# One stream over the quarters in layer 0, whole tiles only in the test of adj, a shorter root, closing algebra by threes

## The chip, the cores and the metric

The kernel runs on one core of a Trainium2 chip. A core has a matmul engine (TensorE, PE in the profile), a vector engine (VectorE, DVE), a scalar engine for activation functions (ScalarE, ACT), a general engine (GpSimd, POOL) and a sync engine (SyncE, SP) that here only issues DMAs. [...] The metric is the device time of one launch in microseconds (us); lower is better. TensorE's clock can be lowered by the chip; in the profiled execution it was granted .984 of full speed on average.

## The reference

There are 4096 nodes with 64 features, a matrix adj of 4096 x 4096 entries of 0 or 1 (a share of .0078 is 1), and four layers of the form x = x + GNN(relu(layernorm(x))):

- Layer 0: a decayed sum over neighbours. `rank` is the running count of neighbours along a row of adj, `k = min(deg, 100)`, `pos = rank - (deg - k)`, and neighbour j counts with `0.5 ** (k - pos)`: the last neighbour has weight 1, the one before 1/2, and so on. `out = w @ (h @ weight) + bias`.
- Layer 1: attention with hyperbolic (Lorentz) linear maps. Such a map computes `h = x @ W.T + b`, `time = sigmoid(h[0]) * exp(scale) + 1.1`, and stretches the other 63 components by `sqrt((time^2 - 1) / sum of squares)`. `att = adj * sigmoid((2 + 2 * qm @ k.T) / att_scale + att_bias)`, then `att @ h`, divided by the root of its Lorentz norm.
- Layer 2: two gated graph convolutions one after the other: `m = adj @ (x @ W)`, then the gates r, z, n of a GRU cell from m and x.
- Layer 3: `adj @ (gamma * X)` and `adj @ (gamma - 1)` for points X of a ball, their quotient, and a chain of norms, artanh and tanh of each node, after which the result is added to x.

The kernel's fast path holds adj in 8-bit floats, which is exact for entries of 0 and 1. So it must also find out whether all entries are 0 or 1: it counts the others, and a general path runs if there are any.

## The kernel before

`fast_kernel` (L791) does the work. Columns of the transposed adj are taken in four quarters of 1024 nodes (`NQ = 4`), each in 32 blocks of 128 rows (`NB = 32`).

**adj comes in twice.** `load0` (L1104; the DMA at L1109) has GpSimd's queue read a tile of 128 x 1024 fp32 and write it as 8-bit floats, 128 KB, to its fixed place in `A8`; 128 tiles in all, 12 before the first turn and then one per turn, 12 ahead. Every later layer reads `A8`. A second full read, on SP's queue, serves the test alone: `checks` (L1060) loads fp32 tiles, and one VectorE operation per tile counts the entries that are neither 0 nor 1. Until layer 2, tiles are halves (128 x 512, 256 KB) in buffers of the pool `b2`, which the rest of the kernel's work shares, four in flight; from layer 2 on there are also wholes (128 x 1024, 512 KB) in the four buffers of `b4`. An order is fixed: the DMAs of a queue are issued in the order written, and so are the tests on VectorE.

**Layer 0.** `stream0(q)` (L1111) is called once per quarter. It goes through the 32 blocks from the last to the first, in pairs. For each block and each half of 512 columns, `turn` (L1117) adds to a running count in PSUM by two matmuls with triangular matrices (`cnt <- A, fupd` and `cnt <- A, ftri`), and the count is turned into a weight tile `w` by ScalarE (three of four) or VectorE (one of four). The sums `acc` over neighbours are matmuls of `w` with the node features, split in a 128-wide part `hm` and a 64-wide `lo`, and stand up to four pairs behind the counts (`waiting`). At the end of a quarter the waiting sums are emptied, `evac` (L1010) copies the sums out at once (two ScalarE copies, two VectorE adds), and only then does the next quarter begin; `post0` does what follows (transposing, adding to x, and the first maps of layer 1). The counts' two PSUM banks are freed at the end of the quarter too.

**Layer 1.** `stream1` (L1310) forms scores by matmul, ScalarE takes their sigmoid, VectorE multiplies with the tile of adj (`sig`), and TensorE sums. One unit of 1024 scores wide takes one of each. Keys of all four quarters must be there before the scores that use them: `k` of quarter q comes from a chain of `relu_ln` (L920), and `lorentz` (L1208) with `stretch` (L1231) twice, mostly small VectorE operations on 128 x 8 elements. All of them use `rsqrt` (L899): a guess from the bits, and three Newton steps of three operations.

**Layers 2 and 3.** Layer 2 runs matmuls of adj with features twice. Layer 3 sums over adj for eight groups u of 512 nodes, (0, 1, 2), (3, 4, 5) and (6, 7); `take3` (L1660) takes the sums of one group from PSUM, and `post3` (L1680) does the closing algebra. `summed` (L1652) hands groups to it in pairs as they come: (3, 4), (5, 0), (1, 2), and 6 and 7 alone.

**The order of the work** is written out when the kernel is built, by a planner, `Weave` (L~640 to 745). It keeps an estimated clock per engine and one for the DMAs (`dma`), and an estimated landing for each loaded tile (`land`: 1.4 us per A tile and per whole, .7 per half). Side work is given as generators in the list `work`, of which two run at a time, and `back`, which holds the tests. After each group of matmuls `draw` issues those operations that can end before TensorE's clock of the plan; `until` and `finish` force them. The estimates only set the order: on the chip engines wait for semaphores.

Engines are wrapped by the class `Engine` (L747), so nearly all operations of ACT, DVE and SP bear line L780, matmuls L946 and transposes L950. Groups in the profile are told apart by the names of their tiles.

Of the kernel before, what the change touches and what calls it, by code (L numbers as in the profile page):

```python
# [9 lines left out]
F32 = mybir.dt.float32  # L10
# [8 lines left out]
P = 128  # L19
D = 64  # L20
# [551 lines left out]
CB = 4  # L572
W0 = float(2.0 ** 27)
# [173 lines left out]
class Engine:  # L747
# [12 lines left out]
    def __getattr__(self, name):  # L760
        fn, w = getattr(self.real, name), self.weave

        def call(*args, **kw):
# [7 lines left out]
            def run():  # L771
# [5 lines left out]
                if name == "dma_start":  # L777
                    for k in outs:
                        w.land(k, 1.4 if "whole" in k else 0.7)
# [11 lines left out]
def fast_kernel(ctx: ExitStack, tc: tile.TileContext, t: dict, out: bass.AP, flag: bass.AP):  # L791
# [18 lines left out]
    b2p = ctx.enter_context(tc.tile_pool(name="fb2", bufs=24))  # L810
    b4p = ctx.enter_context(tc.tile_pool(name="fb4", bufs=4))
    small = ctx.enter_context(tc.tile_pool(name="fsmall", bufs=24))
# [18 lines left out]
    def stat(name, n):  # L831
        return small.tile([P, 2 * QB], F32, tag="st", name=name)[:, :n]
# [66 lines left out]
    def rsqrt(v, eng):  # L899

        n = v.shape[1]
        guess = small.tile([P, 2 * QB], I32, tag="st", name="guess")[:, :n]
        yield eng.tensor_scalar(guess, v.bitcast(I32), -0.5, float(0x5f3759df), op0=ALU.mult, op1=ALU.add)
        y = guess.bitcast(F32)
        for _ in range(3):
            a = stat("nt", n)
            yield eng.tensor_tensor(a, y, y, ALU.mult)
            if eng is DV:
                yield DV.scalar_tensor_tensor(a, a, -0.5, v, op0=ALU.mult, op1=ALU.mult)
                z = stat("ny", n)  # L910
                yield DV.scalar_tensor_tensor(z, a, 1.5, y, op0=ALU.add, op1=ALU.mult)
            else:
                yield eng.tensor_tensor(a, a, v, ALU.mult)
                yield eng.tensor_scalar(a, a, -0.5, 1.5, op0=ALU.mult, op1=ALU.add)
                z = stat("ny", n)
                yield eng.tensor_tensor(z, a, y, ALU.mult)
            y = z
        return y

    def relu_ln(x, dst):  # L920
# [6 lines left out]
        eng = root[0]  # L927
        yield eng.tensor_scalar(v, v, 1.0 / D, LN_EPS, op0=ALU.mult, op1=ALU.add)
        r = yield from rsqrt(v, eng)
        yield DV.scalar_tensor_tensor(dst, xc, 0.0, rows(r), op0=ALU.max, op1=ALU.mult)  # L930

    root = [DV]
# [77 lines left out]
    def evac(acc, bias=None):  # L1010
# [4 lines left out]
        for ps, (own, other) in zip(acc, sides):  # L1015
            S_.activation(mt[own, :], ps[other, :], AF.Copy)
        for ps, (own, other) in zip(acc, sides):
            if bias is None:
                V.tensor_tensor(a[own, :], ps[own, :], mt[own, :], ALU.add)
            else:  # L1020
                V.scalar_tensor_tensor(a[own, :], ps[own, :], bias[own, :], mt[own, :], op0=ALU.add, op1=ALU.add)
# [35 lines left out]
    depth = [4]  # L1057
    spare = [0]

    def checks():  # L1060

        todo = [(b, c) for c in range(NQ) for b in range(NB)]
        loaded, halves, n = [], [], 0

        def load(a, b, c, k):
            Y_.dma_start(a, adjT[b * P:(b + 1) * P, c * CW:(c + k) * CW])
            loaded.append(a)

        while todo or loaded or halves:
            while todo or halves:  # L1070
                whole = sum(a.shape[1] > CW for a in loaded)
                if whole < spare[0] and todo:
                    b, c = todo.pop(0)
                    load(b4p.tile([P, 2 * CW], F32, tag="b4", name="whole"), b, 2 * c, 2)
                elif len(loaded) - whole < depth[0]:
                    if not halves:
                        b, c = todo.pop(0)
                        halves += [(b, 2 * c), (b, 2 * c + 1)]
                    load(b2("half", (P, CW)), *halves.pop(0), 1)
                else:  # L1080
                    break
# [8 lines left out]
        r = stat("odd", 1)  # L1090
        yield DV.tensor_reduce(r, odd, AX.X, ALU.add)
# [743 lines left out]
```

## Time and profile before

| | us |
|---|---|
| three runs | 837.53, 838.41 (median), 840.33 |
| span of the profiled execution | 837.9 |
| TensorE, VectorE, ScalarE busy | 786.7 (94%), 648.4 (77%), 400.8 (48%) |
| 156 tests of halves on VectorE | 101.5, .686 each |
| 50 tests of wholes on VectorE | 59.8, 1.219 each |
| from issue to landing: half, whole, A tile | 6.6, 6.0, 13.3 (medians) |
| DMA queues, 16 engines' share of the span | 30.4% SP's main queue, 21.2% GpSimd's |

Layer 0 takes about 0 to 253 us of the span, layer 1 to 512, layer 2 to 720, layer 3 to 814, and the closing algebra the rest. How to read the profile: a row of a group names line, engine and operation, then "out<-in" by the program's tiles with shapes and the count; after the bar busy time and mean duration in ns, then how long the engine idled just before these instructions and what ended most of that. In a timeline a row begins with start and busy time, and square brackets give the wait ahead of it and what it waited for. In a list of waits, a row gives the waiting work, what it waited for, the sum in us, the count and the longest. An engine that idles off the critical path costs nothing; what counts is what TensorE waits for until its last matmul, and what VectorE does after it.

### The profile page before, as it was taken

How to read it: one execution, taken by the hardware profiler on the slowest of the kernel's cores; microseconds unless marked ns; L12 is line 12 of the kernel's file. 1: busy time of each engine (PE TensorE's matmuls, PEld its weight loads, DVE VectorE, ACT ScalarE, POOL GpSimd, SP SyncE). 2: the span in 40 equal slices, each digit the busy share in tenths (PEclk: the TensorE clock that was granted, in tenths of full speed). 3: DMA queues.
4: the chain of work that ended last, by engine and by line, in shares of the span. 5: the costliest groups of instructions: out<-in, count | busy, mean ns of one | idle time of the engine just before them, and what ended most of it. 6: DMA issues, size and time to landing. Idle time of an engine off the chain costs nothing.

```text
span 837.9 us, 12661 instructions
## 1 busy us (share of the span) xinstructions
PE 786.7 (94%) x4549; PEld 368.7 (44%) x4570; DVE 648.4 (77%) x1675; ACT 400.8 (48%) x613; POOL 69.5 (8%) x143
## 2 busy tenths in 40 slices
PE   5999979999999989999999999999999999999980
PEld 2443423433443333333333333444444444699980
DVE  6535856767688798888888888968778788775995
ACT  4655545555556657566666563122210244462342
POOL 4333232332000000000000000000000000000000
PEclk9999989999999999999999999999999999999995
DMA  9999999999943032002012125596878900000000
GB/s 133 115 146 160 174 184 206 164 179 203 198 124 105 13 105 87 24 26 84 19 51 87 39 57 194 181 314 218 289 242 311 280 26 1 1 2 2 14 22 22
DMA packets 67735, 100.58 MB, mean 120 GB/s; under 512 B 18896, under 2 KB 35280, under 8 KB 67664
## 3 DMA queue, kind: packets, MB, share of 16 engines
q1 hardware_dynamic: 47360, 79.18, 30.4%
q0 software_dynamic: 18432, 16.79, 21.2%
q10 hardware_dynamic: 1872, 3.71, 1.2%
q8 instruction: 38, 0.62, 0.3%
q14 instruction: 33, 0.27, 0.1%
HBM read 144.75 MB, written 5.24 MB: 179 GB/s over the span
## 4 chain that ended last, share of the span: by engine, by line
PE 82%; DVE 9%; DMA 5%; ACT 2%; issue 1%; SPq 0%; DVEq 0%
PE acc L946 50%; PE score L946 13%; PE cnt L946 11%; DMA half<-in_adjT 4%; PE ps_l L946 2%; DVE sig L780 2%; PE rz L946 2%; PE ih L946 2%; PE ps_t L950 1%; DVE nt L780 1%; DVE n L780 1%; DMA x<-in_x 1%; DVE ss L780 1%; ACT w L780 1%; ACT sig L780 1%
## 5 line engine op out<-in xcount | busy, mean ns | idle before, releaser
L780 ACT ACTIVATE sig<-score,fatt_add,fatt_mul 128x1024 f32<-128x1024 f32 x128 | 147.6, 1200 | 82.6 <-PE score L946 82.5
L780 DVE TENSOR_TENSOR sig<-sig,A 128x1024 f32<-128x1024 f32 x128 | 151.3, 1222 | 33.0 <-ACT sig L780 32.6
L780 ACT ACTIVATE w<-cnt 128x512 int16<-128x512 f32 x192 | 108.2, 595 | 100.1 <-PE cnt L946 99.6
L946 PE MATMUL score<-qd,kT 64*128 64x512 f32 x512 | 127.4, 615 | 0.0
L946 PE MATMUL acc<-sig,S 128*64 128x512 f32 x512 | 124.7, 606 | 1.5 <-DVE sig L780 1.5
L946 PE MATMUL acc<-A,hm 128*128 128x512 fp8e4 x512 | 115.6, 379 | 0.0
L946 PEld LDWEIGHTS <-hm 128*128 128x128 bf16 x768 | 73.3, 98 | 91.1 <-issue 12.8
L946 PE MATMUL cnt<-A,fupd 128*128 128x512 fp8e4 x248 | 96.2, 388 | 12.7 <-ACT w L780 6.4
L780 DVE SCALAR_TENSOR_TENSOR half<-half 128x512 f32<-128x512 f32 x156 | 101.5, 686 | 8.0 <-DMA half<-in_adjT 7.9
L946 PE MATMUL cnt<-A,ftri 128*128 128x512 fp8e4 x256 | 98.5, 388 | 8.1 <-DMA A<-in_adjT 8.1
L946 PE MATMUL acc<-S,A 128*128 128x196 bf16 x1024 | 88.2, 247 | 0.0
L946 PEld LDWEIGHTS <-A 128*128 128x128 fp8e4 x1024 | 87.2, 97 | 1.1 <-issue 0.8
L1109 POOL DMA_DIRECT2D A<-in_adjT x128 | 67.7, 531 | 142.5 <-DMA A<-in_adjT 138.4
L946 PEld LDWEIGHTS score<-qd,kT 64*128 64x128 f32 x512 | 44.0, 186 | 79.0 <-issue 36.1
L780 DVE TENSOR_SCALAR w<-cnt 128x512 int16<-128x512 f32 x64 | 44.3, 691 | 41.3 <-PE cnt L946 40.6
L946 PE MATMUL acc<-w,hm 128*128 128x512 bf16 x235 | 69.9, 382 | 0.7 <-issue 0.2
L946 PEld LDWEIGHTS acc<-sig,S 128*64 128x64 f32 x512 | 30.6, 136 | 80.8 <-issue 31.2
L946 PEld LDWEIGHTS <-lo 128*64 128x64 bf16 x768 | 36.9, 109 | 58.5 <-issue 36.7
L780 DVE SCALAR_TENSOR_TENSOR whole<-whole 128x1024 f32<-128x1024 f32 x50 | 59.8, 1219 | 3.0 <-DMA whole<-in_adjT 2.6
L946 PE MATMUL acc<-A,lo 128*64 128x512 fp8e4 x512 | 59.3, 380 | 0.0
L780 ACT ACTIVATE mt<-acc 64x512 f32<-64x512 f32 x32 | 18.9, 591 | 65.6 <-PE acc L946 65.2
L946 PEld LDWEIGHTS <-ftri 128*128 128x128 bf16 x256 | 25.0, 99 | 48.8 <-issue 26.9
(177 smaller groups left out, 684.4 us busy)
## 6 DMA issues: line engine op xcount, KB each, us to landing
half<-in_adjT SPq DMA_DIRECT2D x156, 256.0 KB, 6.6
whole<-in_adjT SPq DMA_DIRECT2D x50, 512.0 KB, 6.0
A<-in_adjT POOLq DMA_DIRECT2D x128, 128.0 KB, 13.3
x<-in_x SPq DMA_DIRECT2D x8, 256.0 KB, 16.6
qd<-qs SPq DMA_DIRECT2D x16, 128.0 KB, 2.7
mx<-gs SPq DMA_DIRECT2D x16, 128.0 KB, 7.3
xT<-gs SPq DMA_DIRECT2D x8, 256.0 KB, 7.0
xs<-x SPq DMA_DIRECT2D x4, 256.0 KB, 7.1
```

The costliest lines, as they stand in the source:

```text
L780: return fn(*args, **kw)
L946: nc.tensor.matmul(o, lhsT, rhs, start=start, stop=stop, skip_group_check=True)
L950: nc.tensor.transpose(o, src, ident)
L1109: nc.gpsimd.dma_start(A8[q][b // 2][:, b % 2, :], adjT[b * P:(b + 1) * P, q * 2 * CW:(q + 1) * 2 * CW])
```

## The change

- `stream0` takes all four quarters in one go. The sums of a quarter may now run on into the turns of the next one; `acc` is kept per quarter, the counts are freed per quarter, and `evac` is no longer done at once but as the first piece of `post0` (and of `post1` in layer 1), among the side work.
- Tests of adj are all of wholes: 128 tiles of 128 x 1024. They are added in the middle of quarter 0 rather than after it, with up to five in flight and, in layer 0, only while the plan's DMA clock is at most 13 us ahead of TensorE's; from the middle of quarter 3 two in flight; in layer 1 no limit by clocks; four in flight after it. Landing estimates go to 1.45 for a tile of A and .8 for other loads.
- Pools: `b2` from 24 to 20 buffers, `b4` from 4 to 6, small buffers from 24 to 22 of wider size (24 columns).
- `rsqrt` has 8 operations: the guess and two longer steps. The Lorentz maps keep `time` less 1 and do with fewer operations (15 to 11 a call). All of it stays on VectorE.
- The closing algebra goes by three: (3, 4, 5), (0, 1, 2), then 6 and 7 alone. Remaining VectorE work of the tests is issued before the last sums of groups 0 to 2; the last extra reduce of the tests is dropped.

The number of TensorE's instructions stays almost the same (8426 instead of 8424 in the two kernels' lists).

```diff
-                        w.land(k, 1.4 if "whole" in k else 0.7)
+                        w.land(k, 1.4 if "whole" in k else 0.8)
...
-    b2p = ctx.enter_context(tc.tile_pool(name="fb2", bufs=24))
-    b4p = ctx.enter_context(tc.tile_pool(name="fb4", bufs=4))
-    small = ctx.enter_context(tc.tile_pool(name="fsmall", bufs=24))
+    b2p = ctx.enter_context(tc.tile_pool(name="fb2", bufs=20))
+    b4p = ctx.enter_context(tc.tile_pool(name="fb4", bufs=6))
+    small = ctx.enter_context(tc.tile_pool(name="fsmall", bufs=22))
...
-    def rsqrt(v, eng):
+    def rsqrt(v):
         n = v.shape[1]
-        guess = small.tile([P, 2 * QB], I32, tag="st", name="guess")[:, :n]
-        yield eng.tensor_scalar(guess, v.bitcast(I32), -0.5, float(0x5f3759df), op0=ALU.mult, op1=ALU.add)
+        guess = small.tile([P, ST], I32, tag="st", name="guess")[:, :n]
+        yield DV.tensor_scalar(guess, v.bitcast(I32), -0.5, float(0x5f3759df), op0=ALU.mult, op1=ALU.add)
         y = guess.bitcast(F32)
-        for _ in range(3):
-            a = stat("nt", n)
-            yield eng.tensor_tensor(a, y, y, ALU.mult)
-            if eng is DV:
-                yield DV.scalar_tensor_tensor(a, a, -0.5, v, op0=ALU.mult, op1=ALU.mult)
-                z = stat("ny", n)
-                yield DV.scalar_tensor_tensor(z, a, 1.5, y, op0=ALU.add, op1=ALU.mult)
-            else:
-                yield eng.tensor_tensor(a, a, v, ALU.mult)
-                yield eng.tensor_scalar(a, a, -0.5, 1.5, op0=ALU.mult, op1=ALU.add)
-                z = stat("ny", n)
-                yield eng.tensor_tensor(z, a, y, ALU.mult)
-            y = z
-        return y
+        a, u, z = stat("nt", n), stat("nu", n), stat("ny", n)
+        yield DV.tensor_tensor(a, y, y, ALU.mult)
+        yield DV.tensor_tensor(u, a, v, ALU.mult)
+
+        yield DV.scalar_tensor_tensor(a, u, -10.0 / 3.0, u, op0=ALU.add, op1=ALU.mult)
+        yield DV.scalar_tensor_tensor(y, a, 5.0, y, op0=ALU.add, op1=ALU.mult)
+        yield DV.tensor_tensor(a, y, y, ALU.mult)
+        yield DV.scalar_tensor_tensor(a, a, -0.5 * (3.0 / 8.0) ** 3, v, op0=ALU.mult, op1=ALU.mult)
+        yield DV.scalar_tensor_tensor(z, a, 1.5 * 3.0 / 8.0, y, op0=ALU.add, op1=ALU.mult)
+        return z
...
         for ps, (own, other) in zip(acc, sides):
-            S_.activation(mt[own, :], ps[other, :], AF.Copy)
+            yield AC.activation(mt[own, :], ps[other, :], AF.Copy)
         for ps, (own, other) in zip(acc, sides):
             if bias is None:
-                V.tensor_tensor(a[own, :], ps[own, :], mt[own, :], ALU.add)
+                yield DV.tensor_tensor(a[own, :], ps[own, :], mt[own, :], ALU.add)
             else:
-                V.scalar_tensor_tensor(a[own, :], ps[own, :], bias[own, :], mt[own, :], op0=ALU.add, op1=ALU.add)
+                yield DV.scalar_tensor_tensor(a[own, :], ps[own, :], bias[own, :], mt[own, :],
+                                              op0=ALU.add, op1=ALU.add)
             free(ps)
...
-    depth = [4]
-    spare = [0]
+    lead = [13]
+    depth = [5]
     def checks():
         todo = [(b, c) for c in range(NQ) for b in range(NB)]
-        loaded, halves, n = [], [], 0
-
-        def load(a, b, c, k):
-            Y_.dma_start(a, adjT[b * P:(b + 1) * P, c * CW:(c + k) * CW])
-            loaded.append(a)
-
-        while todo or loaded or halves:
-            while todo or halves:
-                whole = sum(a.shape[1] > CW for a in loaded)
-                if whole < spare[0] and todo:
-                    b, c = todo.pop(0)
-                    load(b4p.tile([P, 2 * CW], F32, tag="b4", name="whole"), b, 2 * c, 2)
-                elif len(loaded) - whole < depth[0]:
-                    if not halves:
-                        b, c = todo.pop(0)
-                        halves += [(b, 2 * c), (b, 2 * c + 1)]
-                    load(b2("half", (P, CW)), *halves.pop(0), 1)
-                else:
-                    break
+        loaded, n = [], 0
+        while todo or loaded:
+            while todo and len(loaded) < depth[0] and not (loaded and weave.dma > weave.t["P"] + lead[0]):
+                b, c = todo.pop(0)
+                a = b4p.tile([P, 2 * CW], F32, tag="b4", name="whole")
+                Y_.dma_start(a, adjT[b * P:(b + 1) * P, c * 2 * CW:(c + 1) * 2 * CW])
+                loaded.append(a)
...
+    def stream0():
+
         cols = [slice(c * CW, (c + 1) * CW) for c in (0, 1)]
-
-        def turn(b):
+        cnt, acc, waiting = [], {}, []
+
+        def turn(q, b):
...
+        def sums():
+
+            if not waiting:
+                return
+            q, b, w0, w1 = waiting[0]
+            if b == NB - 1:
+                acc[q] = [one(f"acc{c}") for c in (0, 1)]
             for c in (0, 1):
-                add_hm(acc, 0, b, c, w0[c], b == NB - 1)
-            add_hm(acc, 0, b - 1, 0, w1[0], False)
-
-        def add_second(b, w0, w1):
-            add_hm(acc, 0, b - 1, 1, w1[1], False)
+                add_hm(acc[q], 0, b, c, w0[c], b == NB - 1)
+            add_hm(acc[q], 0, b - 1, 0, w1[0], False)
+            yield
+            add_hm(acc[q], 0, b - 1, 1, w1[1], False)
             for i, wt in enumerate((w0, w1)):
                 for c in (0, 1):
-                    add_lo(acc, 0, b - i, c, wt[c], b - i == 0)
-
-        waiting = []
-
-        def sums():
-
-            if not waiting:
-                return
-            item = waiting[0]
-            add_first(*item)
-            yield
-            add_second(*item)
+                    add_lo(acc[q], 0, b - i, c, wt[c], b - i == 0)
             waiting.pop(0)
+            if b == 1:
+                weave.add(post0(q, acc.pop(q)))
         def here(item):
-            part = 0, item[0] // QB
+            part = 0, item[1] // QB
             return part in DONE and weave.ready("P", names(LO[part])) <= weave.t["P"]
-        for b in range(1, NB, 2)[::-1]:
...
+        for q in range(NQ):
+            cnt[:] = [two(f"cnt{c}")[:, :CW] for c in (0, 1)]
+            for b in range(1, NB, 2)[::-1]:
...
+                if b == NB // 2 + 1:
+                    xq[q] = b2(f"x{q}")
+                    Y_.dma_start(xq[q], x_nm[:, q * QB:(q + 1) * QB, :])
+                    if q == 0:
+                        weave.add(checks(), back=True)
+                    if q == NQ - 1:
+                        load1(0)
+                        depth[0] = 2
+            for x in cnt:
+                free(x)
+        begin1()
         while waiting:
             for _ in sums():
                 weave.draw()
...
-    def post0(q, a):
+    def post0(q, acc):
         X = xq.pop(q)
+        a = yield from evac(acc, w("b0"))
...
+        t2, f = stat("t2", n), stat("f", n)
+        yield DV.scalar_tensor_tensor(t2, tm, 2.0, tm, op0=ALU.add, op1=ALU.mult)
+        yield DV.scalar_tensor_tensor(ss, ss, 1e-8, t2, op0=ALU.max, op1=ALU.mult)
+        r = yield from rsqrt(ss)
+        yield DV.tensor_tensor(f, t2, r, ALU.mult)
...
+        yield DV.tensor_scalar(o[:, :, 0], tm, 1.0, sign, op0=ALU.add, op1=ALU.mult)
...
+        while weave.back and weave.back[0][1].e == "D":
+            weave.issue(weave.back[0])
...
+        group.append((u, parts3))
+        if alone or len(group) == 3:
+            weave.add(post3(group[:]))
+            group.clear()
...
-        weave.add(post0(q, evac(acc, w("b0"))))
-        if q == 0:
-            weave.add(checks(), back=True)
+    stream0()
+    lead[0] = math.inf
+    stream1()
     depth[0] = 4
-    stream1()
-    depth[0], spare[0] = 3, 4
     gate_w = []
```

## The prediction

> **What bounds the kernel now.** I read the page first (busy times, slices, chain), then the trace by stages (windows), then TensorE's waits in layer 0, then the timeline around each, last the end.
>
> ```profile
> span 837.9 us, 12661 instructions
> PE 786.7 (94%) x4549; PEld 368.7 (44%) x4570; DVE 648.4 (77%) x1675; ACT 400.8 (48%) x613; POOL 69.5 (8%) x143
> PEclk9999989999999999999999999999999999999995
> 0.00:253.00 253.00, 229.91 (x1141) 98.61 (x1164) 168.99 (x496) 136.78 (x250) 68.58 (x135) 0.99 1.04 167
> 253.00:512.00 259.00, 255.83 (x1112) 84.46 (x1108) 221.42 (x378) 165.78 (x166) 0.00 (x0) 1.00 0.20 58
> 512.00:720.00 208.00, 207.44 (x1240) 95.08 (x1239) 170.24 (x418) 52.96 (x89) 0.46 (x4) 1.00 0.61 201
> 720.00:814.00 94.00, 93.56 (x1063) 90.59 (x1060) 73.30 (x312) 38.23 (x98) 0.46 (x4) 1.00 0.03 7
> 814.00:838.00 24.00, 0.00 (x0) 0.00 (x0) 14.41 (x75) 7.07 (x13) 0.00 (x0) 0.60 0.10 26
> ```
>
> The five lower lines are layer 0, layer 1, layer 2, layer 3 and the tail (sum, then PE, PEld, DVE, ACT, POOL; clock; DMA share; GB/s). TensorE is the bound: all but full in layers 2 and 3, 3 us short in layer 1, 23 us in layer 0, absent from the tail. Only these gaps and the tail can give time; so I ask which wait ends each.
>
> ```profile
> PE cnt L946 <- DMA A<-in_adjT: 8.1, 1, 8.1
> PE cnt L946 <- ACT w L780: 6.4, 11, 1.4
> PE cnt L946 <- DVE w L780: 6.2, 3, 4.0
> ...
> 71.95 0.38 PE L946 MATMUL cnt<-A,fupd 128*128 128x512 fp8e4 x1 [1.37 <-ACT w L780]
> ...
> 95.69 43.04 SPq L780 DMA_DIRECT2D half<-in_adjT  x18
> ...
> 112.24 0.69 DVE L780 SCALAR_TENSOR_TENSOR half<-half 128x512 f32<-128x512 f32 x1 [4.83 <-DMA half<-in_adjT]
> ...
> 113.60 0.59 PE L946 MATMUL cnt<-A,fupd 128*128 128x512 fp8e4 x1 [4.02 <-DVE w L780]
> ...
> 174.96 0.69 DVE L780 SCALAR_TENSOR_TENSOR half<-half 128x512 f32<-128x512 f32 x1 [2.45 <-DMA half<-in_adjT]
> ...
> 307.33 0.66 PE L950 MATMUL ps_t<-fident,k 128*128 128x128 f32 x4 [2.15 <-DVE k L780]
> ...
> 814.42 0.60 DVE L780 TENSOR_TENSOR n<-n,acc 128x130 f32<-128x130 f32 x2
> ...
> 830.40 0.42 DVE L780 TENSOR_TENSOR X<-X,n 128x256 f32<-128x256 f32 x1
> ```
>
> The first wait (8.1) is the start of the kernel; the diff leaves it. The 1.37 us gap at 71.95 is the turn from quarter 0 to 1 and comes again near 136 and 196. The 4.02 us gap is no arithmetic: VectorE stood 4.83 us at a test whose half tile had not landed, with `w` queued behind it. At 307.33 TensorE waits for layer 1's keys. After the last matmul a chain of small VectorE operations runs to 830.8; the output's DMA and the end take 7.1 us more.
>
> [...] `w`, whose counts were ready, stands behind the half. [...] Here the 4.02 us gap is followed by matmuls started .38 to .43 us apart until 118.9 instead of .2155; the 1.37 us gaps show nothing of it. [...] tiles of A land 1.45 us apart alone, 1.91 to 2.02 with halves queued.
>
> **Part 1, one stream over the quarters.** It removes the draining of sums and the immediate evacuation at three turns. From start to start the three boundaries lose 1.54 + .41 = 1.95 us each, 5.85 in all. The evacuation's 2 ACT copies (.59 each) and 2 VectorE adds per quarter stay, but woven between `w` evictions; I leave .3 us per turn for a late `w`. Gain 5.85 − .9 = 4.9 (bounds 0 and 5.85).
>
> **Part 2, tests of whole tiles, earlier, limited.** 156 half tests x .686 = 107.0 us of VectorE become 78 whole tests x (1.219 + .082 spacing) = 101.5: nothing on the path by itself. What counts is where a test waits. The gap at 113.60 costs 4.18 from start to start and about 2.7 at the half clock; that near 176 costs 1.65. Together 8.55. In the changed order SP issues a whole as soon as the test six before it freed a buffer; no load waits for TensorE or ScalarE any longer (halves shared the 2 KB buffers with their work). Issue to test is 5 to 6 pairs of turns, 16 to 20 us. A half landed 16.5 us after issue in the bad spot, about 8 of them in line, 2.05 us per 256 KB, so a whole takes about 4.2 us of the queue under contention, and the limit holds fewer in line. I take the whole 8.55 as gained (bounds 3, if the clock recovers but gaps of a few tenths spread; 8.55; the case of nothing gained is a rival).
>
> Its price is paid by A. Loads start about 23 us earlier: SP can issue six wholes right behind the load of x at 27.5, where the first half went at 50.6. At 28 us about 13.5 tiles of A have landed and 10.5 are used; margins from landing to use are 8.5 us at tile 16, 12.5 at 28, 16.8 at 32. With a whole beside each tile I estimate 2.5 us per tile [...] against a use of about 2 us. Until tile 30 to 38 that consumes the margin and leaves a shortage between 0 and 2.5 us; POOL's loads stay 12 ahead. I take 1.0 lost (bounds 0 and 5). The bytes up to the last A tile stay much the same, so A still ends near 223 us, needed at 240. What is left for layer 2: 74 wholes x 1.30 = 96 us of VectorE beside 208 us in which it was busy 170, instead of 37 halves and 50 wholes = 93.5: covered by TensorE's 207.44 busy of 208.
>
> **Part 3, root of 8 operations instead of 10, shorter algebra.** In layers 1 and 2 it lies beside matmuls, except for the keys at 307.33: lost there 2.44 from start to start, and .99 + .54 us at two other gaps. The key chain loses two operations in relu-layernorm and four in each of two Lorentz maps, 10 x .20 us (start to start of a 128x8 operation) = 2.0; also quarter 3's keys now stand one score unit earlier in the queues, and no whole test stands in that chain. Against it, a unit of 3.79 us holds 2 x 1.22 + 1.30 = 3.74 of VectorE when a whole falls in it. Gain 2.4 (bounds 0 and 3.4). As layers 2 and 3 have no gap, this and parts 1 and 2 pass to the end undiminished.
>
> **Part 4, pools.** 20 instead of 24 buffers of 2 KB (halves no longer use them), 6 of 4 KB, 22 small ones of wider size. Cost nothing: hidden by TensorE's full stages; below zero or above it I see no row (bounds 0 and 1 lost, small-buffer waits in the tail).
>
> **Part 5, closing algebra by groups of three.** VectorE is saturated from 773.6 to 830.8. The sum of before: five groups x 5.2 fixed + eight blocks x 2.95 + takes 7.85 = 57.5, measured 57.2. After: four groups (3,4,5), (0,1,2), 6, 7 x 4.8 (the 8-operation root saves .4), 23.6 for the blocks, 7.05 of takes, one last test with its reduce 1.7; but the first group waits for block 5's take and starts 776.9. 776.9 + 1.7 + 7.05 + 19.2 + 23.6 = 828.4. It is also bounded from TensorE's end: block 7's take, then its own group: 813.6 + .8 + 14.66 − .8 root and one reduce with add ≈ 828.8 or a little more. Gain against 830.84 about 1.6 once TensorE's gains come out of both (bounds 0 and 2.05): the last group's chain moves with TensorE's end, while the VectorE sum moves only with the takes, which wait on TensorE too.
>
> **Sum.** 4.9 + 8.55 − 1.0 + 2.4 + 1.6 = 16.4; 837.9 − 16.4 = 821.5 on the profiled execution. That span stands .5 under the median 838.41 (837.53 to 840.33): 822.0.
>
> **Rivals.**
> (1) A starves. Six wholes at 27.5 us meet the smallest margins, before TensorE can gate anything. For it: margin 8.5 us at tile 16, landing 2.5 against use 2.0. Against: halves at 50.6 already slowed tiles to 1.97 without a wait. If the shortage is 5 and the 1.37 us turns stay half: 822 + 4 + 1.5 ≈ 827.
> (2) The stall only moves. VectorE keeps its order, so a whole that lands late holds `w` as a half did. For it: five wholes are 2.5 MB in flight, four halves 1 MB. Against: nothing on SP waits for the buffers of others, and the limit. 8.5 lost again: ≈ 830.
> (3) No change: the landings govern layer 0 whatever is issued (DMA busy 1.04 of it by the windows), A itself ends late, and parts 3 and 5 return 4 of what is lost: 838 less 1 or so. Against: A's end has 16 us in hand.
> (4) Slower: wholes land later than their tests. Place: tests at pairs 15 to 19, issued 16 to 20 us before. At 4.2 us per whole, test 10 is about 1 us late; it decides above about 6 us per whole, six in line against the packets of A. At 6.2, test 10 lands near 99 instead of 76.5; some 22 us lost in several stops, the half clock with them, less the 14 of gains elsewhere and no 8.55: ≈ 846. For it: a page of DMA slices at 9 throughout layer 0. Against: halves took 2.05 per 256 KB at worst.
>
> **How the numbers follow.** Forecast .60; rival 1 .15; 2 .12; 3 .05; 4 .08. The forecast's own range is 814 (all upper bounds: 5.85 + 8.55 + 3.4 + 2.05 = 19.85, and a few us of `w` waits of ScalarE, 6.4 in all, of which a part goes) to 827. With rivals 1 and 2 the range is 814 to 833; outside it lie rivals 3 and 4 and a little of the rest, under .2. About .3% (2.5 us) is what a measurement of this kernel can tell from no change: faster .87, same .05, slower .08.
>
> **What would show it.** Right: no PE gap of 1.3 us or more between quarters; no stop of VectorE above 2 us at a whole in layer 0, PE spacing at .2155 throughout 100 to 120; layer 0's last count matmul some 12 us earlier; the k wait under .5 us; last VectorE operation 14 to 15 us after the last matmul. Wrong: a `cnt` wait on A's DMA beyond the first 8.1 (rival 1), a wait of a whole for DMA in 60 to 180 us with `w` behind it (2, or 4 if it repeats), or k waiting still. The step I trust least is the share of the queue that a whole takes beside A.

## The result, and the profile after

The changed kernel takes 824.87 us (median of four runs, 824.4 to 825.17) against 839.37 for the kernel before on the same chip: a ratio of .9828, 95% interval .9806 to .985. The forecast was 822.0. The profiled executions have spans of 823.2 and 837.9 us, 14.7 apart.

First the page after: span, busy times, and TensorE's granted clock in 40 slices. Then the windows by stage, with edges moved to where the stages now lie (columns as before: sum, PE, PEld, DVE, ACT, POOL; clock; DMA share; GB/s), and TensorE's waits over the whole span (sum in us, count, longest).

```profile
span 823.2 us, 12224 instructions
PE 786.9 (96%) x4570; PEld 367.6 (45%) x4570; DVE 625.3 (76%) x1393; ACT 398.0 (48%) x607; POOL 69.8 (8%) x143
PEclk9999999999999999999999999999999999999995
```

```profile
0.00:245.00 245.00, 232.45 (x1182) 99.74 (x1184) 157.56 (x373) 139.63 (x253) 68.85 (x135) 1.00 1.02 164
245.00:500.00 255.00, 253.31 (x1094) 82.92 (x1094) 214.83 (x312) 164.04 (x163) 0.00 (x0) 1.00 0.16 52
500.00:708.00 208.00, 206.66 (x1228) 93.71 (x1225) 169.17 (x362) 51.78 (x86) 0.46 (x4) 1.00 0.65 220
708.00:800.00 92.00, 92.00 (x1045) 88.96 (x1043) 68.53 (x272) 35.10 (x91) 0.47 (x4) 1.00 0.02 6
```

```profile
PE cnt L940 <- DMA A<-in_adjT: 8.0, 1, 8.0
PE cnt L940 <- DVE w L781: 3.0, 4, 1.5
PE acc L940 <- DVE sig L781: 1.6, 2, 0.9
PE cnt L940 <- ACT w L781: 1.3, 4, 0.6
PE acc L940 <- DVE X L781: 0.8, 1, 0.8
PE rz L940 <- ACT r L781: 0.4, 1, 0.4
```

TensorE's work is the same (786.9 us busy after 786.7), and it fills 96% of the span instead of 94%. Of layer 0's waits, those on `w` fell from 12.6 us to 4.3; the wait for `k` is gone; two small ones in layer 2 (`X`, `r`) are new. The clock's row no longer dips: the digit 8 in the sixth slice of before is a stretch of 6.8 us at a granted clock of .50, from 112.15 to 118.97, around the end of the 4.02 us stop (113.60).

Stage ends can be compared by the last matmul of each kind, since these do not depend on where a window is cut: the last `acc<-w` for layer 0, the last `acc<-sig` for layer 1, the last `acc<-A` for layer 2, the last `acc<-S` for layer 3.

| end of | before | after | gained in the stage |
|---|---|---|---|
| layer 0 | 256.83 | 244.84 | 12.0 |
| layer 1 | 514.88 | 501.84 | 1.05 |
| layer 2 | 719.55 | 708.24 | −1.7 |
| layer 3 (last matmul) | 813.56 | 802.52 | −.3 |
| last VectorE operation, from last matmul | 17.26 | 15.23 | 2.0 |
| end of span, from last VectorE operation | 7.08 | 5.45 | 1.6 |

So the total is what was forecast within 3 us, and layer 0 (some 12 us were forecast) within 1. Whether it came about by the steps of the forecast is another question, and there the experiments decide.

### The profile page after: what moved, and what is told of

Read it like the earlier page. It is cut to its first block, busy times and chain, and to the rows that moved or that the text cites. A ratio compares the mean times of both kernels' runs of the same rounds, so it can differ in the third digit from the quotient of the medians.

```text
span 823.2 us, 12224 instructions
## 1 busy us (share of the span) xinstructions
PE 786.9 (96%) x4570; PEld 367.6 (45%) x4570; DVE 625.3 (76%) x1393; ACT 398.0 (48%) x607; POOL 69.8 (8%) x143
## 4 chain that ended last, share of the span: by engine, by line
PE 86%; DVE 7%; DMA 3%; ACT 2%; issue 1%; SPq 0%; POOL 0%; DVEq 0%; ACTq 0%; POOLq 0%
PE acc L940 52%; PE score L940 13%; PE cnt L940 12%; DMA whole<-in_adjT 3%; PE ps_l L940 2%; PE rz L940 2%; DVE sig L781 2%; PE ps_t L944 2%; PE ih L940 1%; DMA A<-in_adjT 1%; DVE ss L781 1%; PE ps_kq L940 1%; DVE nt L781 1%; ACT sig L781 1%; PE ps_n L944 0%
## 5 line engine op out<-in xcount | busy, mean ns | idle before, releaser
L781 DVE SCALAR_TENSOR_TENSOR whole<-whole 128x1024 f32<-128x1024 f32 x128 | 153.1, 1219 | 9.5 <-DMA whole<-in_adjT 8.7
L940 PEld LDWEIGHTS <-hm 128*128 128x128 bf16 x768 | 73.2, 98 | 91.1 <-issue 12.6
L940 PE MATMUL acc<-w,hm 128*128 128x512 bf16 x256 | 75.5, 379 | 0.0
L940 PEld LDWEIGHTS <-fupd 128*128 128x128 bf16 x248 | 24.3, 98 | 44.5 <-issue 22.3
```

Source lines behind the costliest of these rows:

```text
L781: return fn(*args, **kw)
L940: nc.tensor.matmul(o, lhsT, rhs, start=start, stop=stop, skip_group_check=True)
```

## The experiments

Four undo one part of the change; two make one part alone in the kernel before; the others follow what these showed. Times are medians; the kernel before took 839.2 to 839.7 beside them. "L0" is the end of layer 0's last matmul as above; "last matmul" is that of layer 3. In two kernels (wholes undone, before + stream) the matmul that sums the count of odd entries comes still later, in the tail.

| kernel | us | L0 | last matmul | from there to the last VectorE operation |
|---|---|---|---|---|
| before | 839.37 | 256.83 | 813.56 | 17.3 |
| changed | 824.87 | 244.84 | 802.52 | 15.2 |
| stream undone | 829.84 | 251.07 | 808.88 | 13.8 |
| wholes undone (halves, late) | 829.18 | 242.53 | 799.73 | 19.7 |
| root and Lorentz maps undone | 837.62 | 250.37 | 810.68 | 19.7 |
| threes undone (pairs) | 826.93 | 244.75 | 802.39 | 17.3 |
| before + stream | 838.51 | 242.14 | 805.06 | 25.2 |
| before + wholes | 840.65 | 258.30 | 816.62 | 17.7 |
| changed, tests late | 824.37 | 241.90 | 799.50 | 17.1 |
| root undone, tests late | 831.13 | 242.32 | 802.16 | 21.0 |
| changed, no limit | 832.27 | 254.36 | 811.43 | 13.8 |
| changed, 6 and 7 together | 822.83 | 245.03 | 802.71 | 12.8 |
| late, no limit, 6 and 7 together | 824.29 | 246.77 | 804.60 | 12.8 |
| late, 6 and 7 together | 821.06 | 242.32 | 799.91 | 14.2 |

**Stream undone.** After each quarter the waiting sums are emptied and the copies made at once.

```diff
...
             for x in cnt:
                 free(x)
-        begin1()
-        while waiting:
-            for _ in sums():
-                weave.draw()
+            if q == NQ - 1:
+                begin1()
+            while waiting:
+                for _ in sums():
+                    weave.draw()
+            weave.add(post0(q, evac_now(acc.pop(q), w("b0"))))
...
```

> The changed kernel with part 1 alone undone: layer 0's sums are emptied and copied out at once at the end of each quarter, all else as changed. Theory (the three turns cost TensorE 1.95 us each and the stream hides all but a few tenths): three PE gaps of 1.3 to 1.4 us before the first cnt matmul of quarters 1, 2, 3, and 5 us more than the changed kernel's 824.9, so 829 to 831. Rival (what paid in layer 0 was only the lost stop at a half; a turn's idle time lets loads of A catch up and is given back later): 824 to 826.5.

Measured 829.84, 4.97 us over the changed kernel. TensorE's waits on ScalarE's `w` are back, with the longest at 1.4:

```profile
PE cnt L940 <- ACT w L781: 6.6, 12, 1.4
```

The last matmul comes 6.4 us later, a little more than the 5.85 us that three turns lost before. The tail gives 1.5 us back, since in this order no test is left for layer 3. The theory holds, the rival (time given back later) falls.

**Wholes undone.** The test generator, pools and landing estimates of before, in the stream, with the tests begun at the end of quarter 0 as before; the early issue of left-over tests in layer 3 is undone as well. The planner's order leaves seven tests after the last take.

```diff
...
-    lead = [13]
-    depth = [5]
+    depth = [4]
+    spare = [0]
...
-                    if q == 0:
-                        weave.add(checks(), back=True)
...
+            if q == 0:
+                weave.add(checks(), back=True)
...
-        while weave.back and weave.back[0][1].e == "D":
-            weave.issue(weave.back[0])
...
-    lead[0] = math.inf
-    stream1()
-    depth[0] = 4
+    depth[0] = 4
+    stream1()
+    depth[0], spare[0] = 3, 4
```

> The changed kernel with part 2 alone undone: halves in the shared buffers until layer 2, tests only from the end of quarter 0, pools of before. Theory A (four halves in line behind A's packets land too late wherever the order puts their tests): stops of VectorE of 2 us or more at a half in layer 0 with w behind, and 831 to 834. Rival B (the 4.02 us stop was the luck of one order, in which one half's load stood late; another order of the same halves has no such stop): no PE gap above 1.5 us in layer 0, and 824 to 828.

Measured 829.18: more than rival B's range and less than A's, so the total decides nothing. The trace does. These are TensorE's waits in layer 0 and the flag's at the end:

```profile
PE flag_ps L940 <- DVE odds L781: 19.3, 1, 19.3
...
PE cnt L940 <- DVE w L781: 1.4, 3, 0.7
```

After the start no wait of TensorE in layer 0 is above .7 us, and VectorE stands at most 1.3 us at a half, with the same halves: rival B is right. Layer 0 ends 2.3 us *earlier* than in the changed kernel. All that this kernel loses it loses at the end, where the count of the odd entries waits for the last tests (19.3 us after the last other matmul). Whether the halves or the missing early issue leave these tests over was not separated.

**Root undone.** `rsqrt` with 10 operations, `lorentz` and `stretch` as before.

```diff
-        a, u, z = stat("nt", n), stat("nu", n), stat("ny", n)
...
+        for _ in range(3):
+            a = stat("nt", n)
+            yield DV.tensor_tensor(a, y, y, ALU.mult)
+            if True:
+                yield DV.scalar_tensor_tensor(a, a, -0.5, v, op0=ALU.mult, op1=ALU.mult)
+                z = stat("ny", n)
+                yield DV.scalar_tensor_tensor(z, a, 1.5, y, op0=ALU.add, op1=ALU.mult)
...
+            y = z
...
```

> The changed kernel with the root of 10 operations and the longer Lorentz maps of before, all else as changed. Theory (only the keys' chain in layer 1 and the closing algebra feel it): a PE wait for k or for what follows from it of 1 to 2.5 us near 290 to 300 us and two roots of the tail .4 us each, so 826 to 828. Rival (layer 1 has slack since the order changed; only the tail's roots count): 825 to 826.

Measured 837.62: 12.7 us more than the changed kernel, and both expectations missed it. The timeline of VectorE and of TensorE (start, busy time, in brackets the wait) and TensorE's wait in layer 1 say why:

```profile
49.74 1.22 DVE L781 SCALAR_TENSOR_TENSOR whole<-whole 128x1024 f32<-128x1024 f32 x1 [3.98 <-DMA whole<-in_adjT]
...
52.28 1.22 DVE L781 SCALAR_TENSOR_TENSOR whole<-whole 128x1024 f32<-128x1024 f32 x1 [1.31 <-DMA whole<-in_adjT]
...
54.04 0.68 DVE L781 TENSOR_SCALAR w<-cnt 128x512 int16<-128x512 f32 x1
```

```profile
54.77 0.58 PE L944 MATMUL cnt<-A,fupd 128*128 128x512 fp8e4 x1 [4.16 <-DVE w L781]
...
57.53 0.63 PE L944 MATMUL cnt<-A,ftri 128*128 128x512 fp8e4 x1
57.96 0.63 PE L944 MATMUL cnt<-A,fupd 128*128 128x512 fp8e4 x1
...
60.78 0.38 PE L944 MATMUL cnt<-A,fupd 128*128 128x512 fp8e4 x1
```

```profile
PE ps_t L948 <- DVE k L781: 4.0, 1, 4.0
```

With other operation counts the lists of the engines come out otherwise. In both kernels the first whole's test stands right behind VectorE's 10th `w`. But in the changed kernel one test stands between the 10th and the 11th `w`, and here there are two. Besides, SP sent the first whole at 32.9 us instead of 30.6. It landed 16.8 us after its issue, as in the changed kernel; VectorE was at the test by 45.8 (45.0 there). So VectorE stood 3.98 us, then 1.31 at the second test, and the 11th `w` came at 54.04; right behind the first test it would have come some 3 us sooner (estimate). TensorE stood 4.16 us for it, and then matmuls started .43 us apart until 60.5, where they had started .22 apart before the stop. This is the stop of the kernel before in another place. Layer 0 ends 5.5 us later by it. Layer 1 takes 3.4 us more, by the keys' wait and 3.4 us of half clock (granted clock .50) behind it, and the tail 4.5 more, with four tests left for layer 3 instead of one.

The late issue has a cause in the queue: the wholes stand behind a load of x, which needs a buffer of the shared pool `b2`. Here is what ended SP's longest wait in the first 33 us, in the changed kernel (first line) and in this one:

```profile
SPq L781 <- PE acc L940: 24.6, 1, 24.6
SPq L781 <- PE acc L944: 26.9, 1, 26.9
```

**Root undone, tests late.** The same, with the tests added to the planner at the end of quarter 0.

```diff
-                    if q == 0:
-                        weave.add(checks(), back=True)
...
             for x in cnt:
                 free(x)
+            if q == 0:
+                weave.add(checks(), back=True)
```

> The changed kernel with the old root and Lorentz maps, as in the run that took 837.6, but with the tests begun at the end of quarter 0. Theory (of that run's 12.7 us more, some 5.5 were a stop at the first whole that the old root's order brought on, not the root): no PE wait above 1 us in layer 0 but the first, last matmul of layer 0 at 241.5 to 243; the wait for k in layer 1 of about 4 us stays (3.4 more than the changed kernel); five tests left in layer 3; in all 829 to 832. Rival (the old root itself slows layer 0): layer 0's last matmul at 247 or later, in all 834 or more.

Measured 831.13. Layer 0 ends at 242.32, no wait on `w` is above .6 us, the wait for `k` is 4.0 us again. So the old root does not slow layer 0; the place of the first tests under it does. Against the changed kernel with late tests (824.37) the root and Lorentz maps are worth 6.8 us: 3.3 in layer 1 (260.26 instead of 256.95), 3.9 between last matmul and last VectorE operation, of which two tests more are some 2.6 (two times 1.30), and small differences elsewhere.

**Threes undone.** `len(group) == 2` in `summed`.

```diff
-        if alone or len(group) == 3:
+        if alone or len(group) == 2:
```

> The changed kernel with groups of the closing algebra by pairs as before: (3,4), (5,0), (1,2), 6, 7. Theory (VectorE is saturated in the tail, and one more group costs its fixed 4.8 us, of which all but what fits in front of block 5's take falls on the end): last VectorE operation 16.5 to 18 us after the last matmul instead of 15.2, 826 to 828. Rival (the end is set by the chain of group 7 alone after its take; groups before it are out of the way by then): 824.5 to 825.5.

Measured 826.93, 2.06 us more. TensorE's stages are the same to .1 us; the last VectorE operation ends 17.27 us after the last matmul instead of 15.23. The theory holds.

**Before + stream, before + wholes.** The two large parts alone, in the kernel before, with its root and pairs. The first takes `stream0`, `post0` and `evac` of the change; the second its `checks`, the pools `b2` and `b4`, limits, landing estimates, and the early issue of left-over tests.

```diff
...
-    for q in range(NQ):
-        acc = stream0(q)
-        weave.add(post0(q, evac(acc, w("b0"))))
-        if q == 0:
-            weave.add(checks(), back=True)
+    stream0()
```

> The kernel before with part 1 alone: one stream over the quarters, its halves, root and pairs kept. Theory (the 4.02 us stop was the luck of one order, and the order of the stream has none; the turns go): no stop of VectorE above 2 us at a half in layer 0, last matmul of layer 0 at 243 to 246 us instead of 256.8. Nine tests are left over for the very end in this order, some 8 us of VectorE after the closing algebra, so in all 831 to 836. Rival (halves in line behind A land too late in any order, so only the turns' 5 us go): a stop of 2 us or more recurs, layer 0's last matmul at 249 to 252, in all 838 or more.

Measured 838.51 (ratio .9976, interval .9961 to .9991). Layer 0 ends at 242.14, 14.7 us earlier than before: the turns and the stop are both gone, with halves. Then it is given back: the wait for `k` grows from 2.2 to 4.0 us, with 6.8 us of half clock from 293.26, and layer 1 takes 3.9 us more, layer 2 2.2, and nine tests stand at the very end:

```profile
PE flag_ps L946 <- DVE odds L780: 24.8, 1, 24.8
...
PE ps_t L950 <- DVE k L780: 4.0, 1, 4.0
```

From the last matmul to the end of the span are 31.9 us instead of 24.3. The theory held for layer 0, and named the leftover tests; what it missed is layers 1 and 2, so the total is above its range.

```diff
...
+                if q == 0:
+                    weave.add(checks(), back=True)
                 if q == NQ - 1:
                     load1(0)
+                    depth[0] = 2
...
+    lead[0] = math.inf
     stream1()
-    depth[0], spare[0] = 3, 4
+    depth[0] = 4
```

> The kernel before with part 2 alone: tests of wholes from the middle of quarter 0, limit, pools of the change. Theory (with the old root the first tests stand after pair 9, before their tiles can land some 17 us after issue, as in the run with the old root): VectorE stops for about 4 us at the first whole near 48 us, half clock after it, turns as before; layer 0's last matmul at 252 to 256, in all 834 to 839. Rival (the forecast's step: wholes as such take the stop away): no stop above 2 us, layer 0's last matmul at 248 to 250, in all 830 to 832.

Measured 840.65 (ratio 1.0014, interval 1.0003 to 1.0025): no gain. The stop only moved:

```profile
52.38 1.23 DVE L780 SCALAR_TENSOR_TENSOR whole<-whole 128x1024 f32<-128x1024 f32 x1 [4.13 <-DMA whole<-in_adjT]
```

```profile
57.48 0.38 PE L946 MATMUL cnt<-A,fupd 128*128 128x512 fp8e4 x1 [4.37 <-DVE w L780]
```

The first whole was sent at 35.4 and landed 17 us later; two tests stand between the 10th and the 11th `w`, as in the run with the root undone. The theory's stop came, but layer 0 ends 1.5 us later than before and the total is above the range: both were put too low. The rival, which was the forecast's own step, falls: wholes as such take no stop away.

**Tests late.** The two hunks shown above, in the changed kernel.

> The changed kernel with the tests begun at the end of quarter 0 instead of its middle, all else as changed. Theory (the early wholes collide with A where its margin is smallest and cost the small waits for w near 48 and 53 us; later ones land in time): no PE wait above 1 us in layer 0 but the first, last matmul of layer 0 at 242 to 243 instead of 244.8; three tests instead of one are left in layer 3, in front of takes; in all 822 to 825. Rival (the start hardly matters to layer 0, and tests moved to the end cost more): 825 to 828.

Measured 824.37. Layer 0 ends at 241.90, 2.9 us earlier, and no wait on `w` is above .6 us. But the reason given was not right: SP's row shows that the first wholes are still sent behind the load of x,

```profile
30.02 0.37 SPq L781 DMA_DIRECT2D x<-in_x  x1
30.43 45.53 SPq L781 DMA_DIRECT2D whole<-in_adjT  x9
```

since six buffers are free and, once x is out, SP sends six without a wait. The loads still go out among those of A, the first at 30.43 us (30.59 in the changed kernel); only the tests stand eight pairs later, behind the 18th `w` instead of the 10th, at 71.13 for the first. What helps is the distance between a load and its test: VectorE comes to the first test 40.7 us after the issue instead of 14.4. The tail takes 1.8 us more, with three tests instead of one in front of takes, so in all only .5 us is left.

**No limit.** `lead = [math.inf]` from the start, in the changed kernel.

> The changed kernel without the limit on the plan's DMA clock in layer 0; tests begin in the middle of quarter 0 as changed, 45 of them before layer 1 instead of 33, and none is left in layer 3. Theory (from quarter 1 on A's tiles have margin enough, and the first ten tests stand as before): the two waits for w near 48 and 53 us and nothing new, last matmul of layer 0 at 244 to 246.5, last VectorE operation 1.7 sooner after the last matmul; in all 822.5 to 825.5. Rival (the limit keeps A from starving): a cnt wait on A's DMA or stops at a whole from 60 us on, layer 0's last matmul at 249 or later, in all 829 or more.

Measured 832.27, 7.4 us more: the rival. Tests after pair 20 come sooner, their loads too, and A starves in quarter 1, with `w` late in other places (the first of three such waits in TensorE's timeline, then the windows from 60 us of this run and of the changed kernel):

```profile
87.42 0.38 PE L940 MATMUL cnt<-A,ftri 128*128 128x512 fp8e4 x1 [0.91 <-DMA A<-in_adjT]
...
```

```profile
60.00:120.00 60.00, 56.04 (x279) 23.47 (x282) 38.40 (x83) 32.38 (x59) 14.78 (x28) 1.00 1.09 213
120.00:180.00 60.00, 58.07 (x293) 24.95 (x298) 44.47 (x112) 33.62 (x64) 17.41 (x33) 1.00 1.10 191
```

```profile
60.00:120.00 60.00, 59.20 (x300) 24.73 (x298) 37.45 (x82) 34.70 (x63) 15.90 (x30) 1.00 1.10 203
120.00:180.00 60.00, 60.00 (x309) 25.77 (x308) 40.19 (x100) 34.43 (x65) 19.61 (x37) 1.00 1.11 168
```

The limit is what made early wholes bearable. The three waits on A (.91 us, .87 at 89.96 and .74 at 94.36) are only 2.5 us of the 9.5 by which layer 0 ends later; the rest is lost in places such as a wait of 1.56 us on `w` at 206. (In the last 70 us before 250 another 3.3 us are missing.)

**6 and 7 together.**

```diff
-            summed(u, take3(u), alone=True)
+            summed(u, take3(u), alone=u == 7)
```

> The changed kernel with groups 6 and 7 of the closing algebra in one call instead of alone. Theory (after the last matmul VectorE goes through two chains of about 7 us, that of 6 having hardly begun; one chain of two blocks takes 4.8 + 2 x 2.95 = 10.7 after the take): last VectorE operation 11.5 to 12.5 us after the last matmul instead of 15.2, in all 821 to 822. Rival (group 6 now starts too late, and what it did beside TensorE is missing): 824 to 827.

Measured 822.83, 2.0 us less than the changed kernel; the last VectorE operation ends 12.8 us after the last matmul. One chain instead of two is right; the total is .8 us above the expected range, the tail .3 us.

**Late, no limit, 6 and 7 together; and the same with the limit.**

> The changed kernel with three edits: tests begun at the end of quarter 0, no limit by clocks, groups 6 and 7 of the closing algebra in one call. No test is left in layer 3. Theory (the savings add: 3.0 us at layer 0's end from the late start, 2.4 in the tail from the one call, 1.8 from the tests that no longer stand in front of takes): last matmul near 799.5, last VectorE operation 12 to 13 us after it, in all 818 to 820. Rival (without the limit the four tests more in layer 0 or the test that moves into layer 1 cost a stop): 821 to 824.

Measured 824.29: the rival's range. The tail is 12.8 us as expected, but TensorE is done at 804.60 instead of 799.5. Layer 0 ends 4.9 us later than with the late start alone; layers 1 to 3 are within .5 us of it. Without the limit the order changed, and TensorE stands for `k` within layer 0:

```profile
232.88 0.82 PE L944 MATMUL ps_t<-fident,k 128*128 128x128 f32 x4 [2.16 <-DVE k L781]
```

The granted clock is at half from 233.2 to 236.6, which costs some 1.7 us more (estimate: half of the 3.4 us), and another wait, for `h1T`, takes .5.

> The changed kernel with two edits: tests begun at the end of quarter 0, the limit kept, and groups 6 and 7 of the closing algebra in one call. TensorE's order is that of the run with the late start alone, instruction by instruction. Theory (what failed in the run with three edits was the order that came with the missing limit): last matmul at 799 to 800, last VectorE operation 14 to 15.5 us after it (three tests stand in front of takes), in all 820 to 822.5. Rival (the tail is full of VectorE work with three tests in it, and one call for 6 and 7 then saves nothing): last VectorE operation 17 us after the last matmul, in all 823.5 to 825.

Measured 821.06 (ratio .978, interval .9765 to .9796), the best of all, 3.8 us under the changed kernel. The last matmul ends at 799.91 and the last VectorE operation at 814.14: the theory holds.

## Why the prediction was right, and where it was not

The forecast's sum was 16.4; the span fell by 14.7. The total is right in part because misses cancel: layer 2 lost 1.7 us and the end of the span gave 1.6, and neither was in the sum. By steps:

- *Part 1, 4.9.* Right in mechanism, and low in size: undoing it delays the last matmul by 6.4 us (4.97 in the time). The copies woven between evictions cost nothing that the trace shows; the .3 us per turn that was kept back was not needed.
- *Part 2, 8.55 gained and 1.0 lost.* The stop did go, and the price was paid, but the step that says why failed. "Issue to test is 5 to 6 pairs of turns, 16 to 20 us", and "no load waits for TensorE or ScalarE any longer": that was to be the cure. It is not. The first six wholes do wait for TensorE, behind the load of x; the first was issued 14.4 us before VectorE stood at its test, and landed after 16.8 (once x had landed, the six came 2.2 to 3.8 us apart, not 4.2). What decides is the place of the tests in VectorE's list. The longest wait of TensorE on VectorE's `w` in layer 0, in us:

| tests | with turns, old root | with turns, new root | stream, old root | stream, new root |
|---|---|---|---|---|
| halves, late | 4.0 (before) | not run | .5 | .7 |
| wholes, early | 4.4 | 1.4 | 4.2 | 1.5 (changed) |
| wholes, late | not run | not run | .4 | .5 |

  With halves the stream moves the tests and takes the stop away. With wholes begun early the stream is neither needed nor enough; there the order that comes with the new root keeps the second test behind the 11th `w`. No step of the forecast led to that: as a reason for the lost stop it is luck. Begun late, wholes stop nothing under either root. Wholes begun early cost layer 0 2.9 us against tests late (the loss that was put at 1.0, by late tests rather than by A's tiles). In layer 0: turns and old stop 14.7 (the stream alone), early tests −2.9, sum 11.8; measured 12.0. At the end, seven tests were left after the closing algebra when halves, their late start and the late issue of left-over tests came back together. That was not in the forecast at all.
- Rival 2, "the stall only moves", had .12. It is what the second part does when it is made alone, and what happens when the root is exchanged. The changed kernel itself came near it: its first whole waits 2.39 us,

```profile
47.43 1.23 DVE L781 SCALAR_TENSOR_TENSOR whole<-whole 128x1024 f32<-128x1024 f32 x1 [2.39 <-DMA whole<-in_adjT]
...
48.58 0.69 DVE L781 TENSOR_SCALAR w<-cnt 128x512 int16<-128x512 f32 x1
...
52.59 1.23 DVE L781 SCALAR_TENSOR_TENSOR whole<-whole 128x1024 f32<-128x1024 f32 x1 [1.32 <-DMA whole<-in_adjT]
```

 and TensorE .87 and 1.46 us for the `w` behind. A second test ahead of the `w` at 48.58 and a later load, and layer 0 lost 5.5 us more in the run with the root undone. The sign "no stop of VectorE above 2 us" at a whole was thus missed by the kernel, though the time was met; so, by a little, was the tail (15.2 us, where 14 to 15 were named).
- *A's landings.* The 2.5 us per tile beside wholes were the author's estimate; in the trace GpSimd's loads, which go as earlier tiles land, stand 2.4 to 2.7 us apart from 49 to 77 us. No `cnt` wait on A but the first: rival 1 did not happen, because of the limit; without it, it does, in part.
- *Part 3, 2.4.* The wait for `k` is gone, and undoing the part costs layer 1 3.3 to 3.4 us. Yet layer 1 itself is only 1.05 us shorter than before. The .99 and .54 us of `acc` waiting for `sig` stay (1.6 us in all, .9 the longest); TensorE's waits in layer 1 fell by 2.1 us, and where the other 1.0 went was not found. And the chain's worth is not the same in both orders: with the old root the wait for `k` is 2.2 us in the order of before and 4.0 in the new one, with 3.4 or 6.8 us of half clock, so undoing shows more than before's trace could.
- *Part 4, 0.* No run changed the pools alone. But in the three kernels with 24 buffers in `b2` the load of x, with the first tests' loads in line behind it, goes out at 26.5 to 27.2 us, and in all with 20 at 29.8 to 35.0. That fits a buffer that comes free one pair of turns or more later, and the forecast had 27.5. What it cost was not measured.
- *Part 5, 1.6.* Measured 2.0 between last matmul and last VectorE operation, about the upper bound of 2.05. The threes alone are worth that much (2.06 when undone).
- *Layer 2, 0.* It lost 1.7 us. The trace has two new waits, .8 for `X` and .4 for `r`; but for the one without the limit (204.70), the experiments have 205.3 to 206.9 us for this layer where the kernel before has 204.67. Which instruction of VectorE's order brings it about stays open.
- *After the last instruction.* 1.6 us were gained between the last VectorE operation and the end, in no step of the forecast. The last output lands 2.5 us after its issue before and 2.4 after. The span from that issue's end is 6.7 us before and 5.0 to 5.2 in all others where no test or flag comes behind that store, even in the kernel before with wholes (839.7 − 834.7). The difference lies in the closing list of SP: between two semaphore instructions it stands from 834.7 to 836.3 in the kernel before, and in the changed one hardly at all (821.5 to 821.6). Its cause was not found.

At the longest stops of layer 0 VectorE kept to the order of its list: a test whose tile has not landed stands at the head (3.98 us the longest wait with the root undone, 4.13 in before + wholes, 4.83 in the kernel before), with `w` behind it. In the kernel before TensorE's last count matmul ahead of the stop started at 109.20 and took .38 us, and the `w` behind the test started at 112.86, after the test (112.24).

## What to carry to other kernels

Where a load's consumer has a fixed place in an engine's list, judge the load by its distance in time from issue to that place: here it lands 16.8 us after issue beside A's tiles. With VectorE at the test 12.8 us after the issue instead of 14.4, and two tests instead of one ahead of the next `w`, layer 0 took 5.5 us more. Look also at what stands ahead of a load in its own queue: here a load of x, for whose buffer SP stood 24.6 to 26.9 us. When parts that look independent share one written order, undo them one by one and make them one by one: here the stream alone gave 0.9 us, the wholes alone lost 1.3, and together with the shorter algebra and the threes they gave 14.5. And look at the tail for what was postponed.

## What the runs showed of the hardware

The half clock did not set in at the moment when work resumed. The list has all stops of TensorE above 2 us in layers 0 and 1 of these traces, except the start; the stretches are those in which the granted clock is .50, in us from the span's start.

| kernel | stop | resumed at | half clock |
|---|---|---|---|
| before | 4.02 | 113.60 | 6.8 from 112.15 |
| before | 2.15 | 307.33 | none |
| root undone | 4.16 | 54.77 | 6.8 from 53.76 |
| root undone | 4.02 | 302.13 | 3.4 from 302.94 |
| before + stream | 4.02 | 293.90 | 6.8 from 293.26 |
| before + wholes | 4.37 | 57.48 | 3.4 from 58.23 |
| before + wholes | 2.16 | 308.80 | none |
| root undone, tests late | 4.02 | 294.08 | 3.4 from 294.59 |
| late, no limit, 6 and 7 together | 2.16 | 232.88 | 3.4 from 233.19 |

So equal stops of 4.02 us were followed by 3.4 or 6.8 us of half clock, and it began up to 1.5 us before work resumed or up to .8 after. All six stops of 4.02 to 4.37 us had such a stretch, and one of three stops of some 2.2 us; stops of 1.56 us and less had none. Every stretch lasted 3.4 or 6.8 us. What decides between the two, and why one stop of 2.16 us had a stretch and another of 2.16 us had none, these runs do not show.
